# Grouping the tiled matmuls of a four-layer graph kernel: scores, the attends of the pair before, and scores as one block of TensorE

## The chip, the cores and the metric

One NeuronCore of a Trainium2 chip runs the whole program. The metric is device time in microseconds (us) of one execution; medians over several executions are given with their range. The profile is one execution taken with the hardware profiler, whose span is some 2 us shorter than the timed execution.

## The reference

Input `x` is 128 batches of 128 nodes by 512 features in float32, `adj` a 128 x 128 matrix shared by all batches. Four layers follow each other, each with a residual and a layer norm: a graph convolution, a graph attention, a max over differences, and masked multi-head attention. The argument concerns the last one.

```python
# layer 3, per batch: n = 128 nodes, d = 512, H = 8 heads of hd = 64
qkv = (x @ w_qkv).reshape(b, n, 3, H, hd).transpose(2, 0, 3, 1, 4)
q, k, v = qkv[0], qkv[1], qkv[2]
attn = jnp.einsum('bhnd,bhmd->bhnm', q, k) * scale          # "scores"
attn = jnp.where(attn_mask[None, None] == 0, -jnp.inf, attn)
attn = jax.nn.softmax(attn, axis=-1)
o = jnp.einsum('bhnm,bhmd->bhnd', attn, v)                  # "attends"
o = o.transpose(0, 2, 1, 3).reshape(b, n, d) @ w_proj + b_proj
# ... return o + layernorm(o)
```

## The kernel before

The kernel does not write its instructions in the order in which it describes them. Each batch is a generator, a *chain*, that asks for an engine for an estimated time; a planner grants the request that could start first, and the order in which it grants them becomes the fixed order of instructions on each engine. The planner's times decide order alone; on the chip, semaphores decide when each instruction runs.

```python
BUFS = {
    "tr": 3, "mm": 3, "sc": 1,                       # PSUM; sc holds one batch's scores, two banks
    "x": 16, "yT": 3, ..., "v": 8, "qkT": 3, "pr": 2, ...
}

def at(self, r):                                      # earliest start of request r
    engine, _, take, _, _ = r["want"]
    t = max(r["ready"] + (min(MARGIN, r["ready"] / 20) if engine == "PE" else 0.0),
            self.free.get(engine, 0.0))
    ...                                               # and not before its buffers come free
    return t

def run(self):
    while self.requests:
        t, _, _, n = min((self.at(r), r["want"][4], r["rank"], n) for n, r in enumerate(self.requests))
        ...
```

Two batches are a group (`G = 2`). The scores of a batch use 64 rows of the array for each head, the attends 64 columns of it. Everything else (products with the weights, `mixed`, `query_key`) uses the whole 128 x 128 array.

```python
def attend(gr, bs):                                   # both batches of a group together
    for b in bs:
        yield gr.rows[b]                              # transposed probabilities have landed
    slots = yield use("PE", 0.25 + 0.88 * len(bs), lambda: ("tr", "oT") * len(bs), late=0.2, urgent=True)
    for n, b in enumerate(bs):
        valued, prT, bt = gr.heads.pop(b)
        p = bank([P, K, P], "tr")
        for c in range(K):
            for j in range(2):
                nc.tensor.matmul(p[j * HD:(j + 1) * HD, c, :],
                    valued.v[:, (2 * c + j) * HD:(2 * c + j + 1) * HD], prT[:, j * K + c],
                    start=True, stop=True)
    ...

def batch(i):
    ...
    yield gr.qk
    bs = yield use("PE", 1.13, "sc", late=0.2, urgent=True)
    sc = bank([P, 2, K, P], "sc")
    for c in range(K):
        for j in range(2):
            rws = slice(j * HD, (j + 1) * HD)
            nc.tensor.matmul(sc[:, j, c, :], gr.qkT[rws, c, nodes], gr.qkT[rws, K + c, nodes],
                start=True, stop=True)
    bpr = yield use("DVE", 1.22, "pr", urgent=True)
    nc.vector.tensor_tensor(pr, sc..., maskb..., op=ALU.add)     # frees sc
    ...                                               # softmax, 32x32 transposes, two DMAs -> prT
    yield gr.attended[b]
    ...                                               # ACT copy oT, projection, DVE: o, layer norm, out
```

## Time and profile before

| | before |
|---|---|
| time, median of 3 runs | 3310.55 us (3310.03 to 3311.14) |
| span of the profiled execution | 3309.2 us |
| TensorE (PE) busy | 99% |
| VectorE (DVE) busy | 80% |
| waits of TensorE for other engines | 13.4 us in all |

How to read it: TensorE is the path, so busy time of other engines costs nothing as long as TensorE doesn't wait for it. The profile's durations of matmuls overlap (a 512-column instruction is drawn 594 ns long on average, and in a stream the next one starts 429 ns after it), so all readings here subtract **start from start**. A float32 matmul of the source is two instructions in the trace, and in an undisturbed stream one of 512 columns takes 429 ns, one of 256 takes 216 and one of 128 takes 112.

### The profile page before, as it was taken

The page shows a single profiled execution, that of the slowest core. Times are in us where ns is not written, and L with a number is a line of the kernel's source. Part 1 is how long each engine was busy: PE and PEld are TensorE (multiplying, and loading weights), DVE is VectorE, ACT ScalarE, POOL GpSimd, SP SyncE. Part 2 cuts the span into 40 slices and gives each one's busy share as a digit, 9 for nine tenths or more (in the row PEclk, how much of TensorE's full clock was granted, in tenths as well). Part 3 has the DMA queues.
Part 4 walks back from the last instruction along what each step waited for, and adds up shares of the span by engine and source line. Part 5 has one row for each costly group of instructions (what it writes and reads, how often), then busy time and mean ns, then how long its engine had stood idle before and what let it go on. Part 6 is the DMA issues. An engine that isn't in the chain of part 4 may idle for free.

```text
span 3309.2 us, 43603 instructions
## 1 busy us (share of the span) xinstructions
PE 3286.0 (99%) x14613; PEld 2060.0 (62%) x14613; DVE 2640.0 (80%) x5527; ACT 1182.6 (36%) x3457; POOL 935.1 (28%) x1031
## 2 busy tenths in 40 slices
PE   9999999999999999999999999999999999999998
PEld 5666566665656565656666665666565656656655
DVE  7877888768987888787787778886887788778876
ACT  2433244332442333333333333433333334343332
POOL 3222322223222333132233233131331242222322
PEclk9999999999999999999999999999999999999999
DMA  4333223332233232223322332323223332322322
GB/s 163 84 111 100 81 71 101 104 90 91 71 108 96 83 91 88 93 78 101 96 80 91 99 88 88 89 84 113 83 61 116 92 94 72 109 82 71 102 83 80
DMA packets 469760, 304.47 MB, mean 92 GB/s; under 512 B 319264, under 2 KB 401312, under 8 KB 469536
## 3 DMA queue, kind: packets, MB, share of 16 engines
q1 hardware_dynamic: 469536, 301.69, 30.5%
q8 instruction: 116, 1.90, 0.3%
q14 instruction: 108, 0.88, 0.1%
HBM read 158.93 MB, written 142.67 MB: 91 GB/s over the span
## 4 chain that ended last, share of the span: by engine, by line
PE 97%; DVE 2%; DMA 1%; issue 0%; POOL 0%; ACT 0%; SPq 0%; POOLq 0%; ACTq 0%; DVEq 0%
PE mm L199 52%; PE mm L470 27%; PE tr L207 7%; PE sc L625 4%; PE tr L499 4%; PE mm L595 3%; DVE e L442 0%; DMA z<-s_d 0%; DVE st L165 0%; DVE scr L567 0%; DVE x L560 0%; DVE x L186 0%; DMA prT<-p_d 0%; DVE et L445 0%; PE tr L315 0%
## 5 line engine op out<-in xcount | busy, mean ns | idle before, releaser
L199 PE MATMUL mm<-w_sb,yT 128*128 128x512 f32 x2048 | 909.6, 594 | 3.1 <-ACT yT L210 2.0
L470 PE MATMUL mm<-xT,wqkv_sb 128*128 128x256 f32 x4096 | 909.3, 380 | 0.0
L470 PEld LDWEIGHTS mm<-xT,wqkv_sb 128*128 128x128 f32 x4096 | 773.6, 190 | 138.3 <-issue 28.3
L172 POOL TENSOR_TENSOR rstd<-ve,neghalf 128x1 f32<-128x1 f32 x640 | 418.2, 654 | 1528.5 <-DVE ve L169 1241.9
L199 PEld LDWEIGHTS mm<-w_sb,yT 128*128 128x128 f32 x2048 | 381.3, 190 | 451.0 <-issue 434.1
L199 PE MATMUL mm<-wqkv_sb,xT 128*128 128x512 f32 x1024 | 465.9, 598 | 0.0
L199 PE MATMUL mm<-wproj_sb,oT 128*128 128x512 f32 x1024 | 457.4, 596 | 1.5 <-ACT oT L675 1.5
L643 ACT ACTIVATE pr<-pr,nmx 128x128 f32<-128x128 f32 x1024 | 397.7, 391 | 139.9 <-DVE nmx L639 139.2
L165 DVE BATCH_NORM_STATS2 st<-x 128x6 f32<-128x512 f32 x512 | 349.2, 682 | 10.4 <-ACT x L603 7.6
L199 PEld LDWEIGHTS mm<-wproj_sb,oT 128*128 128x128 f32 x1024 | 193.7, 191 | 231.0 <-issue 222.4
L192 POOL TENSOR_TENSOR x<-x,o 128x512 f32<-128x512 f32 x128 | 175.3, 1370 | 533.7 <-DVE o L683 532.6
L199 PEld LDWEIGHTS mm<-wqkv_sb,xT 128*128 128x128 f32 x1024 | 189.1, 190 | 200.3 <-issue 189.8
L181 ACT ACTIVATE x<-x,nmr,rstd 128x512 f32<-128x512 f32 x256 | 205.9, 809 | 279.0 <-DVE nmr L179 270.7
L632 DVE TENSOR_TENSOR pr<-sc,maskb 128x1024 f32<-128x1024 f32 x128 | 156.2, 1220 | 156.1 <-PE sc L625 155.8
L210 ACT COPY yT<-tr 128x512 f32<-128x512 f32 x256 | 148.8, 584 | 262.6 <-PE tr L207 262.2
L192 POOL TENSOR_TENSOR x<-x,beta_sb 128x512 f32<-128x512 f32 x128 | 172.6, 1351 | 201.2 <-DVE xt L609 181.3
L519 ACT COPY v<-mm 128x512 f32<-128x512 f32 x128 | 74.8, 584 | 427.8 <-PE mm L199 427.5
L478 ACT ACTIVATE qkT<-mm 128x512 f32<-128x512 f32 x128 | 76.3, 596 | 371.9 <-PE mm L470 371.8
L192 POOL TENSOR_TENSOR x<-x,bias_sb 128x512 f32<-128x512 f32 x128 | 176.3, 1387 | 106.5 <-PE tr L207 95.8
L567 DVE SCALAR_TENSOR_TENSOR scr<-x,wa_rows 128x512 f32<-128x512 f32 x256 | 195.1, 762 | 13.9 <-ACT x L181 8.8
L643 ACT ACTIVATION_READ_ACCUMULATOR pr<-pr,nmx 128x1 f32 x1024 | 193.4, 189 | 0.0
L625 PEld LDWEIGHTS sc<-qkT 64*128 64x128 f32 x2048 | 124.2, 187 | 81.9 <-issue 65.0
(64 smaller groups left out, 3539.1 us busy)
## 6 DMA issues: line engine op xcount, KB each, us to landing
p_d<-pt SPq DMA_DIRECT2D x128, 512.0 KB
prT<-p_d SPq DMA_DIRECT2D x128, 512.0 KB
x<-in_x SPq DMA_DIRECT2D x128, 256.0 KB
x_d<-xt SPq DMA_DIRECT2D x128, 256.0 KB
xT<-x_d SPq DMA_DIRECT2D x512, 64.0 KB
out<-x SPq DMA_DIRECT2D x128, 256.0 KB
z<-s_d SPq DMA_DIRECT2D x64, 128.0 KB
e_d<-et SPq DMA_DIRECT2D x64, 128.0 KB
```

The costliest lines, as they stand in the source:

```text
L165: nc.vector.bn_stats(st, src)
L172: nc.gpsimd.tensor_tensor(rstd, ve, neghalf, op=ALU.pow)
L181: nc.scalar.activation(xb, xb, AF.Identity, bias=nmr, scale=rstd)
L192: nc.gpsimd.tensor_tensor(dst, dst, other, op=ALU.add)
L199: nc.tensor.matmul(p, lhs(k), rhs(k), start=(k == 0), stop=(k == K - 1))
L207: nc.tensor.matmul(p[:, k, :], xb[:, k * P : (k + 1) * P], nodes, start=True, stop=True)
L210: nc.scalar.copy(yT, p)
L470: nc.tensor.matmul(p[:, j, :], wqkv_sb[:, k, (c + j) * P : (c + j + 1) * P], gr.xT[:, k, :], start=(k == 0), stop=(k == K - 1),)
L567: nc.vector.scalar_tensor_tensor(scr, xb, 1.0, wa_rows[:, j, :], op0=ALU.mult, op1=ALU.mult, accum_out=gr.s[:, b, j : j + 1],)
L625: nc.tensor.matmul(sc[:, j, c, :], gr.qkT[rws, c, nodes], gr.qkT[rws, K + c, nodes], start=True, stop=True,)
L632: nc.vector.tensor_tensor(pr, sc.rearrange("p j c m -> p (j c) m"), maskb[:, None, :].to_broadcast([P, H, P]), op=ALU.add,)
L643: nc.scalar.activation(pr[:, j, :], pr[:, j, :], AF.Exp, bias=nmx[:, j : j + 1], accum_out=sums[:, j : j + 1],)
```

## The change

The intent: the scores of a pair's first batch, the attends of the pair before, and the scores of its second batch follow each other directly, so that the array leaves its whole-array mode once per pair in place of three times. The attends in the middle give VectorE time to empty the only score buffer. A request with `follow=True` goes ahead of others that could start at the same time, and `at()` plans it without its margin (not shown). A block without other work in it is called *undivided* below, and a step from whole-array work into a block an *entry*. Two buffer counts change too. The last eight batches (`TAIL`) keep single scores.

```diff
-    "x": 16, "yT": 3, ..., "v": 8, "qkT": 3,
+    "x": 16, "yT": 4, ..., "v": 6, "qkT": 3,
+TAIL = 8
-        return engine, work, names, late, not urgent
+        return engine, work, names, late, 0 if follow else 1 if urgent else 2
...
+    def tiled(gr, before, bs=range(G)):
+        yield gr.qk
+        if before:
+            for b in range(G):
+                yield before.rows[b]
+        got = yield use("PE", 1.1 if len(bs) == 1 else 1.0,
+            lambda: ("sc",) + ("pr",) * len(bs) + ("tr", "oT") * (G if before else 0),
+            late=0.0, urgent=True)
+        gr.pr.extend(got[1 : 1 + len(bs)])
+        score(gr, bs[0], got[0])
+        if before:
+            yield use("PE", 0.88 * G + 0.15, late=0.0, follow=True)
+            attends(before, range(G), got[1 + len(bs) :])
+        for b in bs[1:]:
+            got = yield use("PE", 1.15, "sc", follow=True)
+            score(gr, b, got)
...
+            if g * G < NB - TAIL:
+                plan.start(tiled(groups[g], groups.get(g - 1)), rank)
+            else:
+                for b in range(G):
+                    plan.start(tiled(groups[g], None, (b,)), rank)
+            if g * G >= NB - TAIL - G:
+                for bs in ((0, 1),) if g * G < NB - G else ((0,), (1,)):
+                    plan.start(attend(groups[g], bs), rank)
... (score() and attends() hold the matmuls of before, unchanged; batch() waits for its scores)
```

More of the change, by code (lines that the diff above doesn't have):

```diff
@@ L30 @@
     "tr": 3, "mm": 3, "sc": 1,
-    "x": 16, "yT": 3, "z": 2, "e": 2, "et": 1, "eT": 2, "ex": 2, "xT": 2, "v": 8, "qkT": 3,
+    "x": 16, "yT": 4, "z": 2, "e": 2, "et": 1, "eT": 2, "ex": 2, "xT": 2, "v": 6, "qkT": 3,
     "pr": 2, "pt": 1, "xt": 2, "prT": 2, "oT": 2, "o": 2,
 }
+TAIL = 8
 MARGIN = 1.0
@@ L56, in __init__, with use @@
         self.now = 0.0
-    def use(self, engine, work, take=None, late=0.05, urgent=False):
+    def use(self, engine, work, take=None, late=0.05, urgent=False, follow=False):
         names = take if callable(take) else lambda: (take,) if take else ()
-        return engine, work, names, late, not urgent
+        return engine, work, names, late, 0 if follow else 1 if urgent else 2
     def start(self, chain, rank):
@@ L90, in at @@
     def at(self, r):
-        engine, _, take, _, _ = r["want"]
-        t = max(r["ready"] + (min(MARGIN, r["ready"] / 20) if engine == "PE" else 0.0), self.free.get(engine, 0.0))
+        engine, _, take, _, order = r["want"]
+        early = min(MARGIN, r["ready"] / 20) if engine == "PE" and order else 0.0
+        t = max(r["ready"] + early, self.free.get(engine, 0.0))
         names = take()
@@ L368, in __init__ @@
             self.rows, self.attended = ([Event() for _ in range(G)] for _ in range(2))
-            self.heads, self.o, self.prT = {}, {}, []
+            self.scored = [Event() for _ in range(G)]
+            self.heads, self.o, self.prT, self.sc, self.pr = {}, {}, [], {}, []
             self.eT, self.xT, self.qkT, self.slot, self.left = {}, None, None, {}, {}
@@ L386, in group @@
                 plan.start(query_key(groups[g], n // 2 * 2 + K * (n % 2)), g * G + n / K - (8 if g * G >= NB - 8 else 0))
-            for bs in ((0, 1),) if g * G < NB - G else ((0,), (1,)):
-                plan.start(attend(groups[g], bs), g * G - (8 if g * G >= NB - 8 else 0))
+            rank = g * G - (8 if g * G >= NB - 8 else 0)
+            if g * G < NB - TAIL:
[6 more added lines that the diff above has]
+                    plan.start(attend(groups[g], bs), rank)
         return groups[g]
@@ L485, in query_key, with score @@
         done(gr.qk)
+    def tiled(gr, before, bs=range(G)):
[3 more added lines that the diff above has]
+                yield before.rows[b]
+        got = yield use(
+            "PE", 1.1 if len(bs) == 1 else 1.0,
+            lambda: ("sc",) + ("pr",) * len(bs) + ("tr", "oT") * (G if before else 0),
+            late=0.0, urgent=True,
+        )
+        gr.pr.extend(got[1 : 1 + len(bs)])
[6 more added lines that the diff above has]
+            score(gr, b, got)
+    def score(gr, b, bs):
+        sc = bank([P, 2, K, P], "sc")
+        nodes = slice(b * P, (b + 1) * P)
+        for c in range(K):
+            for j in range(2):
+                rws = slice(j * HD, (j + 1) * HD)
+                nc.tensor.matmul(
+                    sc[:, j, c, :], gr.qkT[rws, c, nodes], gr.qkT[rws, K + c, nodes],
+                    start=True, stop=True,
+                )
+        gr.read("qkT", G)
+        gr.sc[b] = sc, bs
+        done(gr.scored[b], 0.15)
     def attend(gr, bs):
@@ L490, in attend, with attends @@
         slots = yield use(
-            "PE", 0.25 + 0.88 * len(bs), lambda: ("tr", "oT") * len(bs), late=0.2, urgent=True
+            "PE", 0.25 + 0.88 * len(bs), lambda: ("tr", "oT") * len(bs), late=0.0, urgent=True
         )
+        attends(gr, bs, slots)
+    def attends(gr, bs, slots):
         for n, b in enumerate(bs):
@@ L507, in attend @@
         for b in bs:
-            done(gr.attended[b])
+            done(gr.attended[b], 0.2)
     def values(i, gr, event):
@@ L615, in batch @@
         plan.start(values(i, gr, valued), i + G)
-        yield gr.qk
-        bs = yield use("PE", 1.13, "sc", late=0.2, urgent=True)
-        sc = bank([P, 2, K, P], "sc")
-        nodes = slice(b * P, (b + 1) * P)
-        for c in range(K):
-            for j in range(2):
-                rws = slice(j * HD, (j + 1) * HD)
-                nc.tensor.matmul(
-                    sc[:, j, c, :], gr.qkT[rws, c, nodes], gr.qkT[rws, K + c, nodes],
-                    start=True, stop=True,
-                )
-        gr.read("qkT", G)
-        bpr = yield use("DVE", 1.22, "pr", urgent=True)
-        pr = buf([P, H, P], "pr")
+        yield gr.scored[b]
+        sc, bs = gr.sc.pop(b)
+        yield use("DVE", 1.22, urgent=True)
+        pr, bpr = buf([P, H, P], "pr"), gr.pr.pop()
         nc.vector.tensor_tensor(
```

## The prediction

> **What bounds the kernel now.** I read four views in this order: the page (busy shares and the chain that ended last), the list of waits of TensorE, the instructions in order of time in the middle of the run, and the same at its end. The page first:
>
> ```profile
> PE 3286.0 (99%) x14613; PEld 2060.0 (62%) x14613; DVE 2640.0 (80%) x5527; ACT 1182.6 (36%) x3457; POOL 935.1 (28%) x1031
> ...
> PE 97%; DVE 2%; DMA 1%; issue 0%; POOL 0%; ACT 0%; SPq 0%; POOLq 0%; ACTq 0%; DVEq 0%
> ```
>
> TensorE is busy for 99% of the span and carries 97% of the chain that ended last; VectorE, the next, is busy for 80%. The TensorE waits for other engines add up to 13.4 us in the whole run, 4.6 of them one wait near the end. So time can only go in two places: in what the stream of matmuls itself costs, and in those few waits. A busy share of 99% does not say that the stream is dense, so I read the starts. Middle of the run, TensorE alone; the columns are start, duration, engine, line, operation, tiles, count (each f32 matmul of the source appears as two instructions):
>
> ```profile
> 1507.23 1.97 PE L499 MATMUL tr<-prT,v 128*64 128x128 f32 x32
> 1509.13 3.72 PE L470 MATMUL mm<-xT,wqkv_sb 128*128 128x256 f32 x16
> 1512.68 3.60 PE L199 MATMUL mm<-wproj_sb,oT 128*128 128x512 f32 x8
> 1516.21 1.16 PE L625 MATMUL sc<-qkT 64*128 64x128 f32 x16
> 1517.30 3.70 PE L199 MATMUL mm<-wproj_sb,oT 128*128 128x512 f32 x8
> 1520.93 1.16 PE L625 MATMUL sc<-qkT 64*128 64x128 f32 x16
> ```
>
> Subtract starts, not durations. The scores (sc, 64 rows of the array) and the attends (prT, 64 columns of it) are tiled; all else uses the whole array. In the trace, 512-column instructions that follow each other start 429 ns apart, so eight are 3.43 us. The eight at 1512.68 stand behind whole-array work and in front of a score: 1516.21 - 1512.68 = 3.53, which is 0.10 more. The eight at 1517.30 stand between two scores: 3.63, which is 0.20 more. Going through the starts of the whole trace, these two costs are the same at every place: the last whole-array instruction before a tiled one takes 94 ns more (523 for 429, 309 for 216, 205 for 112), and the first after one takes 104 ns more (533 for 429, 320 for 216). **A visit of whole-array work between two tiled blocks costs 198 ns besides its work.** Within the tiled blocks nothing depends on the neighbour: a score block takes 1092 ns from its first start to the next block's first start in all 128 cases, the 16 behind attends included; an attend block of a pair 1898 ns before a whole-array block and before a score alike.
>
> **The Trainium skill** says in "TensorEngine Tiling (Array Packing)", section Key Properties, that changing the tiling mode drains the TensorE. The trace agrees, and gives a size: 94 + 104 ns around a whole-array visit. By the same sentence score next to attend (row tiles next to column tiles) is a change of mode too; the trace agrees, since the score behind attends still takes 1092 ns, so that boundary is not free, it only lacks the 198. "Perfetto Trace Analysis", section Identifying the Most-Contended Engine, warns that matmul busy share is no measure of headroom; here 198 ns holes are hidden inside a 99%. "TensorE: Matmul & The Clock Gate", Part 1: The HAM clock gate, says that an idle stretch of about 3.4 us halves the clock; the end of the run shows that, below.
>
> **The change, part by part.**
>
> (1) Switches. No matmul is added or removed; the blocks only move. I counted the order of TensorE instructions in both built programs. Entries from whole-array work into tiled work: before 112 into scores and 64 into attends, 176 in all (111 scores and 49 attend blocks stand alone). After: 95 and 6, 101 in all. The intent, scores, attends, scores undivided for each pair, is met in only 33 places; in 26 the block is scores, attends, then other work, then the second scores; 36 scores stand alone, being those second ones and the last groups. So 176 - 101 = 75 visits fewer, each worth 198 ns: **75 x 0.198 = 14.9 us off the path**, all of it on TensorE, which is the path.
>
> (2) The end. The same view there, and the granted clock in windows of it (columns: window, length, busy time and count, clock, DMA share, GB/s):
>
> ```profile
> 3272.60 1.16 PE L625 MATMUL sc<-qkT 64*128 64x128 f32 x16
> 3273.69 7.13 PE L199 MATMUL mm<-wproj_sb,oT 128*128 128x512 f32 x16
> 3285.42 1.44 PE L499 MATMUL tr<-prT,v 128*64 128x128 f32 x16 [4.60 <-DMA prT<-p_d]
> 3287.59 6.30 PE L199 MATMUL mm<-wproj_sb,oT 128*128 128x512 f32 x8 [0.73 <-ACT oT L675]
> 3293.82 1.09 PE L499 MATMUL tr<-prT,v 128*64 128x128 f32 x16
> 3295.66 3.70 PE L199 MATMUL mm<-wproj_sb,oT 128*128 128x512 f32 x8 [0.74 <-ACT oT L675]
> ```
>
> ```profile
> 3280.80:3285.40 4.60, 0.03 (x1) 1.00 0.45 132
> 3285.40:3287.60 2.20, 1.44 (x17) 0.64 0.32 132
> 3287.60:3293.80 6.20, 6.20 (x8) 0.58 0.60 200
> ```
>
> After the last scores only 7.1 us of other work is left, while softmax, transposing and two transfers of the probabilities need 11.7 us (3273.7 to 3285.4): TensorE waits 4.6 us. Then its clock is at 0.58, and eight instructions take 6.2 us in place of 8 x 0.429 = 3.4, so the wait costs 4.6 + 2.7 = 7.3 us. In the changed order, after the last scores stand eight value products, the attends of a pair, four more and eight projection products: 20 source matmuls of 512 columns (two instructions each) at 0.858 us, and 1.9 us, 19.1 us in all. That covers 11.7 us. **I expect the wait and the slow clock behind it to go: 7.3 us.**
>
> (3) A new wait. The scores have one PSUM buffer. In an undivided block the second scores need VectorE to have read the first, while only the attends lie between. From the last start of the first scores: 0.20 to the attends plus 1.90 for them is 2.10 us. VectorE begins the mask addition 0.32 us after that start when it is free (median of 128) and takes 1.22: it ends at 1.54, so 0.56 us is to spare, somewhat less with the signal. In the trace of before, VectorE began over 0.53 us after in a quarter and over 1.02 us in a tenth of the cases; it overruns beyond some 0.8. With 33 such blocks, an estimated 10 to 20% late by some 0.5 us, it costs 2 to 3 us. The 26 divided blocks have no such wait: other work stands there.
>
> (4) Buffers. Six v for eight: at most six products are in v or being made in the changed order, five before, so it fits with nothing over. Attends that wait for the next pair's scores lengthen every batch's life: counted in the order, a median of 11 batches are open, after 9 (most 15, after 14, of 16 x buffers). Adding up matmul durations between the last projection of one batch and the first use of its x buffer by another leaves at least 23 us in the changed order, 74 before. In before, with 74, the earliest use came 64 us after the load's issue; so some 12 us remain in the worst case. Enough, with little over; I put 1 us there. Fourth yT: removes at most the few waits for other work in the middle (1 to 2 us each, three of them); I expect them to come and go, and count 0.
>
> Sum: 3310.6 - 14.9 - 7.3 + 2.5 + 1 = 3291.9; I leave a little for the 2.1 us wait for ScalarE at 3207.7, where more work now stands between, and say **3291 us**.
>
> **The rivals.** (a) The stall in the block takes the gain back. For it: one score buffer, VectorE at 80%, a fixed order that was planned with rounded durations. Were all 33 blocks late by 0.5 us, that is 16 us, and the time is 3305. Against it: the order put other work in the 26 places where the buffer would be late, and the one undivided block of before had no wait. (b) The score-attend boundary costs more than the parts say, since I have 16 cases of attend to score, but only one of score to attend (201 ns, and then the usual attend block). If it hid a drain of 100 ns, 59 such boundaries give 6 us back: 3297. (c) The longer life of a batch starves the first layer of x or the end of work: each stall over 3.4 us also costs clock, as the end of before shows; two would make 3305. (d) The end does not improve, or has another long wait: 3298. None makes VectorE or the DMA queues the bound: their work is unchanged.
>
> **Range and chances.** The 14.9 is counted, and sure within 1 or 2 us unless (b) holds; the 7.3 is likely; the losses are 0 to 10. That gives 3284 to 3301. A change of 2% is 66 us, over four times the switches saved, and a loss of that size would need stalls of 1 us per pair everywhere: 98% for within 2%.
>
> **What will show it.** Fewer entries into tiled work, each still 94 and 104 ns, and attends starting 0.20 us after the last start of scores with no extra; TensorE busy some 15 to 18 us less; no wait of 4.6 us and no clock under 1 at the end; waits of the second scores for the mask addition, a few us in total. Wrong it would be if that wait is frequent, if a wait for the x load or for prT appears in the middle, or if the boundary of scores and attends turns out dear.

## The result

| | before | changed |
|---|---|---|
| time, median of 4 runs | 3310.85 us (3310.03 to 3311.89) | 3292.85 us (3292.42 to 3293.42) |
| span of the profiled execution | 3309.2 us | 3291.2 us |
| ratio | | 0.9946 (0.9928 to 0.9963) |

A ratio here is the mean time of one kernel's fast runs over that of the other's in the same rounds, so it is not quite the ratio of the medians quoted. The time fell by 18.0 us, 0.54%: within 2%, and 1.9 us above the predicted 3291. The output is correct.

The page of the changed kernel, to set against the two lines of before:

```profile
PE 3269.0 (99%) x14613; PEld 2064.7 (63%) x14613; DVE 2663.6 (81%) x5527; ACT 1186.9 (36%) x3457; POOL 965.6 (29%) x1031
...
PE 95%; DVE 3%; DMA 1%; SPq 1%; issue 0%; ACT 0%; POOL 0%; POOLq 0%; DVEq 0%; ACTq 0%
```

The same 14,613 matmuls are busy for 17.0 us less, and the chain that ended last has 3% of VectorE where it had 2%. TensorE in order of time, in the middle of the changed kernel (start, duration, engine, line, operation, tiles, count):

```profile
1464.74 3.62 PE L485 MATMUL mm<-xT,wqkv_sb 128*128 128x256 f32 x16
1468.29 1.16 PE L528 MATMUL sc<-qkT 64*128 64x128 f32 x16
...
1572.45 1.16 PE L528 MATMUL sc<-qkT 64*128 64x128 f32 x16
1573.54 1.97 PE L551 MATMUL tr<-prT,v 128*64 128x128 f32 x32
1575.44 1.16 PE L528 MATMUL sc<-qkT 64*128 64x128 f32 x16
```

An undivided block: 1573.54 - 1572.45 = 1.09 us for the scores and 1575.44 - 1573.54 = 1.90 for the attends. These are the 1092 and 1898 ns that the same blocks took alone. Before a block nothing changed either: 16 instructions at 216 ns are 3.46 us, and 1468.29 - 1464.74 is 3.55, the 94 ns of the entry. The end of the changed kernel, in the same columns:

```profile
3247.20 1.16 PE L528 MATMUL sc<-qkT 64*128 64x128 f32 x16
3248.29 7.13 PE L205 MATMUL mm<-wqkv_sb,xT 128*128 128x512 f32 x16
3255.36 1.97 PE L551 MATMUL tr<-prT,v 128*64 128x128 f32 x32
3257.26 3.70 PE L205 MATMUL mm<-wqkv_sb,xT 128*128 128x512 f32 x8
3260.79 7.03 PE L205 MATMUL mm<-wproj_sb,oT 128*128 128x512 f32 x16
3267.75 1.09 PE L551 MATMUL tr<-prT,v 128*64 128x128 f32 x16
3269.59 3.70 PE L205 MATMUL mm<-wproj_sb,oT 128*128 128x512 f32 x8 [0.74 <-ACT oT L716]
...
3275.05 3.70 PE L205 MATMUL mm<-wproj_sb,oT 128*128 128x512 f32 x8 [0.74 <-ACT oT L716]
```

From 3248.29 to 3267.75 there is 19.5 us of other work behind the last scores, and the attends of the last pair start with no wait. Eight projection instructions take 3.6 us, so the clock is full. The list of TensorE's waits (engine, tile and line, for what, us in total, times, longest) starts with the new one:

```profile
PE sc L528 <- DVE pr L673: 3.0, 3, 1.3
PE mm L205 <- ACT oT L716: 2.1, 3, 0.7
PE tr L213 <- DMA eT<-e_d: 1.5, 1, 1.5
```

Two of the three waits for the mask addition are in undivided blocks (1.36 and 1.35 us by starts, at 1883.3 and 2445.6 us). The third, 0.50 us at 169.4, is in a divided block, where the prediction expected none.

**Where the 18 us went.** I went through all starts of both traces. Each step from start to start was split into its undisturbed length, 94 ns if a tiled block follows, 104 ns if one preceded, and whatever is left (waits and slow clock). All numbers are us of the profiled execution.

| | entries into tiled work | x 0.198 | undisturbed work | waits, slow clock | after the last matmul's start | span |
|---|---|---|---|---|---|---|
| before | 176 | 34.8 | 3243.6 | 18.9 | 10.4 | 3309.2 |
| changed | 101 | 20.0 | 3243.3 | 13.5 | 13.0 | 3291.2 |
| difference | -75 | -14.8 | -0.3 | -5.4 | +2.6 | -18.0 |

(1.4 us before the first matmul is in the span of both.) The undisturbed work is what is left of the time to the last start, so it should agree, as both kernels do the same matmuls. That it does within 0.3 us says that the steps at entries are alike in both traces; it is a check of the bookkeeping and not a test of its own, as a longer step would have been booked as a wait. What tests the 0.198 are the runs below that add and remove entries.

The -5.4 is a net: the wait for the probabilities with its slow clock is gone (-7.6), a wait of 2.2 us for ScalarE shortly before is gone, second scores wait for the mask addition (+3.2 by starts), and some others came (+1.2). The +2.6 was not predicted: from the last matmul's start to the end of the program, the changed kernel takes 13.0 us and the kernel before 10.4.

VectorE at the end of the changed kernel, in order of time:

```profile
3278.71 0.75 DVE L736 SCALAR_TENSOR_TENSOR x<-t,rstd,x 128x512 f32<-128x512 f32 x1
3279.49 0.69 DVE L171 BATCH_NORM_STATS2 st<-x 128x6 f32<-128x512 f32 x1
3280.22 0.18 DVE L173 BATCH_NORM_AGGREGATE mv<-st 128x2 f32<-128x6 f32 x1
3280.44 0.15 DVE L175 TENSOR_SCALAR ve<-mv 128x1 f32<-128x1 f32 x1
3280.51 0.68 DVE L724 TENSOR_TENSOR o<-mm,bproj_sb 128x512 f32<-128x512 f32 x1
3281.32 1.49 DVE L192 TENSOR_SCALAR x<-x,mv,rstd 128x512 f32<-128x512 f32 x1
3282.74 0.68 DVE L171 BATCH_NORM_STATS2 st<-o 128x6 f32<-128x512 f32 x1
```

The last product ends at about 3278.75. Its bias addition (L724) starts at 3280.51, because four VectorE instructions of the batch before stand ahead of it in the fixed order. In the kernel before, the last product ended at 3299.36 and the addition started at 3300.03. From the last matmul's start that is 2.35 us against 1.26, and makes 1.1 of the 2.6 us. The other 1.5 come right after it: the scaling of the batch before (L192) stands between the addition and its statistics, which so begin 2.23 us after the addition's start, and 0.72 us in the kernel before. This scaling took 1.49 us beside an addition to x by GpSimd (3281.27, 1.26 us); in this trace the same operation took 503 to 547 ns in all 211 places where no such addition ran beside it, and up to 1644 ns in the 45 where one did. So part of the gain at the end is lost again in VectorE's order of work.

### The profile page after: what moved, and what is told of

Read it like the earlier page. It is cut to its first block, busy times and chain, and to the rows that moved or that the text cites. A ratio compares the mean times of both kernels' runs of the same rounds, so it can differ in the third digit from the quotient of the medians.

```text
span 3291.2 us, 43479 instructions
## 1 busy us (share of the span) xinstructions
PE 3269.0 (99%) x14613; PEld 2064.7 (63%) x14613; DVE 2663.6 (81%) x5527; ACT 1186.9 (36%) x3457; POOL 965.6 (29%) x1031
## 4 chain that ended last, share of the span: by engine, by line
PE 95%; DVE 3%; DMA 1%; SPq 1%; issue 0%; ACT 0%; POOL 0%; POOLq 0%; DVEq 0%; ACTq 0%
PE mm L205 51%; PE mm L485 27%; PE tr L213 6%; PE sc L528 4%; PE tr L551 3%; PE mm L647 3%; DVE st L171 0%; SPq L589 0%; DMA z<-s_d 0%; DVE x L640 0%; DVE x L192 0%; DVE x L612 0%; DMA s_d<-s 0%; DVE mv L173 0%; DVE pr L691 0%
## 5 line engine op out<-in xcount | busy, mean ns | idle before, releaser
L178 POOL TENSOR_TENSOR rstd<-ve,neghalf 128x1 f32<-128x1 f32 x640 | 444.1, 694 | 1521.8 <-DVE ve L175 1267.0
L205 PE MATMUL mm<-wqkv_sb,xT 128*128 128x512 f32 x1024 | 455.6, 593 | 0.0
L691 DVE TENSOR_TENSOR pr<-pr,rs 128x1024 f32<-128x1024 f32 x128 | 192.0, 1500 | 4.4
```

The costliest lines, as they stand in the source:

```text
L178: nc.gpsimd.tensor_tensor(rstd, ve, neghalf, op=ALU.pow)
L205: nc.tensor.matmul(p, lhs(k), rhs(k), start=(k == 0), stop=(k == K - 1))
L691: nc.vector.tensor_tensor(pr, pr, rs[:, :, None].to_broadcast([P, H, P]), op=ALU.mult)
```

## The experiments

Twelve runs on the chip follow, two of them repeats (r_after is the changed kernel, r_old_buffers is e2_old_buffers). The budget above was drawn up for each, and belongs to all experiments:

| run | entries | x 0.198 | undisturbed | waits, slow clock | after last start | span | time, median |
|---|---|---|---|---|---|---|---|
| e1_buffers | 187 | 37.0 | 3243.4 | 27.8 | 10.1 | 3319.7 | 3321.64 |
| e2_old_buffers | 101 | 20.0 | 3243.6 | 13.4 | 10.1 | 3288.5 | 3288.54 |
| e3_no_follow | 192 | 38.0 | 3243.5 | 24.7 | 10.1 | 3317.7 | 3319.11 |
| e5_split | 223 | 44.2 | 3252.0 | 21.9 | 11.5 | 3330.9 | 3330.63 |
| e6_twice | 178 | 35.2 | 3358.0 | 20.6 | 10.1 | 3425.2 | 3427.0 |
| e7_forced | 76 | 15.1 | 3243.6 | 39.1 | 10.1 | 3309.2 | 3310.00 |
| e8_end | 101 | 20.0 | 3243.5 | 15.7 | 11.4 | 3292.0 | 3291.62 |
| e9_close | 93 | 18.4 | 3243.7 | 14.1 | 11.4 | 3289.0 | 3291.89 |
| r_after | 101 | 20.0 | 3243.4 | 12.5 | 13.0 | 3290.4 | 3292.91 |
| r_old_buffers | 101 | 20.0 | 3243.6 | 10.9 | 10.1 | 3286.0 | 3288.06 |
| e10_end_pair | 100 | 19.8 | 3243.5 | 9.5 | 12.7 | 3286.9 | 3288.63 |
| e11_end_both | 100 | 19.8 | 3243.5 | 9.7 | 12.9 | 3287.3 | 3289.07 |

The theory is that of the prediction: a visit of whole-array work between tiled blocks costs 198 ns, and the gain is the number of visits saved plus the end. The rivals: the buffers do it, the place of the attends does it, or the gaps are no real time.

### The buffers alone, and the order alone

```diff
 # e1_buffers: the kernel before with
-"yT": 3, "v": 8
+"yT": 4, "v": 6
 # e2_old_buffers: the changed kernel with
-"yT": 4, "v": 6
+"yT": 3, "v": 8
```

> The kernel before, with the two buffer counts of the change alone (four yT, six v). Its order has 187 entries from whole-array work into tiled work, against 176 before and 101 after. Theory (the switches and the end make the gain, not the buffers): 11 x 0.198 = 2.2 us slower for the switches, and a longer wait for the probabilities at the end, since only one value product stands after the last scores: some 4 to 8 us more. About 3317 us, 3311 to 3322; each entry still 94 and 104 ns. Rival (the fourth yT takes waits away and makes the gain): 3300 us or less.

> The changed kernel with the old buffer counts (three yT, eight v). Its order again has 101 entries into tiled work, 32 undivided blocks for 33, and the same last steps. Theory: the same time as the changed kernel within 3 us, 3290 to 3296. Rival (the buffers matter): 3300 or more.

The buffers alone made the kernel slower: 3321.64 us (3320.84 to 3321.88), 1.0027 of before (1.0012 to 1.0042). Entries are +2.2 us as counted, and most of the rest is the end, where the wait for the probabilities is 12 us. TensorE there, in order of time:

```profile
3295.93 1.98 PE L499 MATMUL tr<-prT,v 128*64 128x128 f32 x16 [12.00 <-DMA prT<-p_d]
```

The new order with the old buffers took 3288.54 us (3287.65 to 3290.33), ratio 0.9928 (0.9914 to 0.9943), 1.5 us below the expected band. So **the order makes the gain, not the buffer counts**, and with the old counts it is larger. To see whether that difference is real, I ran both on one chip, five rounds each:

> The changed kernel again, on the same chip as the next two, for a fair comparison of the buffer counts. Both theories: 3292.9 us within 2 us.

> The changed kernel with three yT and eight v again. Theory (its 4 us are the 2.9 us of VectorE's order at the end and chance between chips): 2 to 4 us under the changed kernel of this call, in the trace all of it after the last matmul's start, none in entries or waits. Rival (the buffers take waits away): TensorE's last start over 2 us earlier than the changed kernel's.

The changed kernel took 3292.91 us (3291.49 to 3293.12), with the old counts 3288.06 (3287.79 to 3289.56); the ranges do not touch, and the difference is more than the 2 to 4 us expected. In all four traces of the two kernels the part after the last start is 13.0 us with the new counts and 10.1 with the old: 2.9 us. VectorE at the end of e2_old_buffers shows the difference; the last matmul started at 3278.42:

```profile
3279.31 0.68 DVE L724 TENSOR_TENSOR o<-mm,bproj_sb 128x512 f32<-128x512 f32 x1
3280.03 0.69 DVE L171 BATCH_NORM_STATS2 st<-o 128x6 f32<-128x512 f32 x1
```

The addition starts 0.89 us after it (2.35 in the changed kernel), and its statistics follow directly. **TensorE has no long wait at the end here either, so the changed kernel's longer end is not the price of the removed wait.** It comes with the order that the plan gave VectorE under the new counts.

The last start itself came 0.3 us later with the old counts in the first pair of traces and 1.5 us earlier in the second. Two differences repeat in both pairs and nearly cancel: by starts, scores wait 0.1 us for the mask addition with the old counts and 3.2 and 2.4 us with the new; in the list of waits, products wait 3.8 and 3.7 us for yT with the old counts and 0.7 with the new. One does not repeat: in e2_old_buffers the clock record reaches full rate at 10.5 us and not at 5.0 as in r_old_buffers, which cost it 1.5 us (e3_no_follow and e8_end have the same). The remainder is in waits that differ from run to run, and is not settled.

### Dividing the blocks again

```diff
-        return engine, work, names, late, 0 if follow else 1 if urgent else 2
+        return engine, work, names, late, 1 if follow or urgent else 2
```

> The changed kernel where the attends and the second scores are asked for as ordinary urgent work, so that whole-array work comes between them: 192 entries into tiled work for 101, one block for 33. Theory: 91 x 0.198 = 18.0 us slower, less the 3.2 us that second scores waited for the mask addition; and its end has one value product after the last scores, so the wait for probabilities comes back there, with the slow clock, some 5 to 10 us: about 3317 us, 3308 to 3322; in the trace 18.0 us of it in starts around entries. Rival (what gained was the place of the attends in the order and the end, not the missing entries): the TensorE stream up to 3200 us into the run is no longer than in the changed kernel by more than 4 us, and the total is under 3303.

Measured: 3319.11 us (3317.33 to 3319.51), inside the expected band. Everything else of the change is kept (the margin of `at()` comes back with the edit), and 18.0 us come back in entries; the "undisturbed" column stays at 3243.5. Another 11 us come back in waits, nearly all of it one: the last scores of this order have one value product behind them, and TensorE waits 12.0 us for the probabilities, followed by slow-clock instructions:

```profile
PE tr L551 <- DMA prT<-p_d: 12.0, 1, 12.0
```

The total alone does not rule out the rival that only the place of the attends mattered, as this wait is part of it. The trace does: what the changed kernel's TensorE has done by 3200.0 us, this one, measured by undisturbed lengths, has done by 3215.1, where the rival allowed 4 us.

### More entries on purpose

```diff
 # the kernel before, with the attends of each batch asked for apart
-for bs in ((0, 1),) if g * G < NB - G else ((0,), (1,)):
+for bs in ((0,), (1,)):
```

> The kernel before with the attends of the two batches of each pair asked for apart: 223 entries into tiled work for 176, 124 attend blocks for 65. Theory: 47 x 0.198 = 9.3 us for entries, and each further attend block has its own first gap (50 ns more) and last gap (99 ns more), 59 x 0.149 = 8.8 us; with a longer wait at the end of some 4 to 8 us about 3335 us, 3328 to 3340. Rival (these starts are how the profiler draws matmuls, and no time lies in them): 3311 to 3319.

Measured: 3330.63 us (3329.15 to 3332.71), inside the expected band. The 47 further entries cost 9.3 us, and the 59 further attend blocks raised the undisturbed column by 8.4 us, where 8.8 was expected. Sixteen-instruction attend blocks take 1024 ns from start to the next block's start, in front of whole-array work and of scores alike. If the gaps were only drawn by the profiler, the time would have stayed near 3311 to 3319. They are time.

### Twice the same mode

```diff
 # the kernel before: each batch's eight score matmuls issued twice, over the same buffer (still correct)
-        for c in range(K):
+        for c in list(range(K)) * 2:
```

> The kernel before with each block of scores computed twice in a row (the same eight matmuls again, over the same buffer; the result stays right), to see whether tiled work behind tiled work of the same mode pays anything. Theory (the extra gaps belong to a change of mode, not to a new group of matmuls): the second eight take 8 x 112 = 896 ns, blocks of 1988 ns for 1092, the stream 128 x 0.896 = 114.7 us longer. Rival (each group of eight pays its own first and last gap): blocks of 2184 ns, 139.8 us. In both cases the end of this order has one value product after the last scores, and so some 8 us more of wait: about 3434 us in the first, 3459 us in the second.

One look: 3427.0 us, state unknown. TensorE in the middle, in order of time:

```profile
1521.40 2.06 PE L625 MATMUL sc<-qkT 64*128 64x128 f32 x32
1523.38 3.70 PE L199 MATMUL mm<-wqkv_sb,xT 128*128 128x512 f32 x8
1527.01 2.06 PE L625 MATMUL sc<-qkT 64*128 64x128 f32 x32
1529.00 1.27 PE L207 MATMUL tr<-eT,x 128*128 128x128 f32 x9
```

A doubled block takes 1.98 us (1985 ns in all 128 cases): 893 more, not 1092. So tiled work behind tiled work of the *same* mode pays nothing, and a block's own extra (1092 - 8 x 112 = 196 ns) belongs to the change of mode. That the second eight use the same operands and buffer is not the reason: the attends of a pair are two batches with two buffers, and their block of 1898 ns is also shorter than two of 1024 (e5_split). Scores next to attends keep that part and lose only the 198 ns.

### Forcing the blocks together

Only 33 of 59 blocks with attends are undivided, because the planner puts other work in where it sees the score buffer come free late. This run lets the second scores follow anyway.

```diff
+    def key(self, r):
+        t, free = self.at(r), self.free.get(r["want"][0], 0.0)
+        return free if r["want"][4] == 0 and t - free < 1.0 else t
...
-                (self.at(r), r["want"][4], ...
+                (self.key(r), r["want"][4], ...
+            t = self.at(r)
```

> The changed kernel, where the second scores of a block may be placed directly after the attends even if the plan sees the score buffer come free up to 1 us late: 76 entries into tiled work for 101, 57 undivided blocks for 33. Theory (a late buffer costs more than the entry that it saves): 25 x 0.198 = 5.0 us saved, but the second scores then wait for the mask addition, 10 to 18 us in total for 3.2; and its end has 8.8 us of work after the last scores for 19.1, so the wait for the probabilities is there again with the slow clock, some 8 us. About 3308 us, 3299 to 3315. Rival (the plan divided too often, the real buffer is in time): waits of second scores under 5 us in total, and without the end's wait a stream shorter than that of the changed kernel by 3 us or more.

Measured: 3310.00 us (3308.31 to 3311.87). Its two largest waits of TensorE:

```profile
PE tr L556 <- DMA prT<-p_d: 12.8, 1, 12.8
PE sc L533 <- DVE pr L678: 8.4, 10, 2.2
```

Entries fell by 5.0 us. Second scores waited 8.4 us in this list, for 3.0 in the changed kernel; by starts it is 10.0 in 17 places, the lower edge of the 10 to 18 expected. By the starts, without the end's 17.7 us (12.9 of wait, a slow clock and two copies by ScalarE), 21.4 us of waits are left; the changed kernel has 11.9 without its two copies. So the forced blocks save 5.0 and the waits rise by 9.5, part of them waits for other things that moved. Dividing a block where the buffer is late was right in this order.

### The end

```diff
 # e8_end: the changed kernel; plans the last bias addition earlier in VectorE's order
-        bp = yield use("PE", 3.46, "mm", late=0.2)        # projection
+        bp = yield use("PE", 3.46, "mm", late=0.2 if i < NB - 1 else -1.8)
 # e9_close: old buffer counts, the line above, and key() as above with 0.15 us, in the first 2000 us
```

> The changed kernel with one thing moved: VectorE's bias addition to the last projection product is placed in VectorE's order ahead of the last statistics of the batch before it. Theory (the 2.6 us more that the changed kernel needs after its last matmul come from VectorE's order there, as the last product now ends while VectorE is busy with the batch before): 1.0 to 1.8 us less after the last matmul's start than the 13.0 of the changed kernel, so about 3291.4 us. Rival (the chain of the last batch itself is what takes that time): 13.0 us as before, 3292.9.

> A try for a better version: the changed kernel with the old buffer counts, a plan that places the second scores directly after the attends when their buffer is at most 0.15 us late (in the first 2000 us only), and the last bias addition moved up as in the run on the end. 93 entries into tiled work for 101. Theory: 8 x 0.198 = 1.6 us less for entries, under 1 us of new waits, and an end like that of the kernel with the old buffers (10.1 us after the last start) or better: 3286 to 3289. Rival (buffer waits eat it, or other waits come): 3290 or more.

e8_end took 11.4 us after the last start in place of 13.0: the expected 1.0 to 1.8 us. Its time, 3291.62 us (3288.82 to 3293.75), agrees with the expected 3291.4, but the runs scatter over more than the effect; the profiled execution had 2.2 us more waits elsewhere (a stretch of 3.4 us at half the clock, behind a wait of 1.9 us at 1885, cost it 1.7 us, and a late full clock at the start 1.6; other waits were shorter). What is shown is the trace's 1.6 us. e9_close saved its 1.6 us of entries, but had an end of 11.4 us where the kernel with the old counts has 10.1 without it, and other waits: 3291.89 us (3289.28 to 3295.55), no better, as its rival said.

```diff
 # e10_end_pair: old buffer counts, and the last pair's attends as one block
-for bs in ((0, 1),) if g * G < NB - G else ((0,), (1,)):
+for bs in ((0, 1),):
 # e11_end_both: e10_end_pair, with late=-1.0 for the last projection
```

> The kernel with the old buffer counts, where the attends of the very last pair are one block too, in place of two with a projection between: 100 entries into tiled work for 101, 64 attend blocks for 65, one wait for ScalarE's copy of 0.81 us for two. Theory: 0.81 + 0.20 + 0.15 = 1.2 us less than the kernel with the old buffer counts in this call. Rival (VectorE's work on the last two batches is the end's bound): no less.

> The kernel with the last pair's attends as one block and the old buffer counts, and with VectorE's bias addition to the last product placed ahead of the scaling of the batch before it. TensorE's order is unchanged by it. Theory (VectorE's order at the end takes back what TensorE saved): after TensorE's last start 10.5 to 11.5 us for 12.7, and so 1 to 2 us less, 3286.5 to 3287.6 where the kernel without it had 3288.6; the best of all. Rival (two batches' work on VectorE does not fit in less): 12.7 us and 3288.6 again.

Both failed as tries for a faster kernel, and the rivals held. In e10_end_pair the TensorE stream is 1.7 us shorter (last start at 3274.2 for 3275.9, on the same chip), with no wait for ScalarE's copy between the last products, and the time is 3288.63 us (3288.33 to 3289.00) for 3288.06. VectorE shows why:

```profile
3274.88 0.84 DVE L733 SCALAR_TENSOR_TENSOR t<-o,mv,gamma_sb 128x512 f32<-128x512 f32 x1
3276.16 0.75 DVE L736 SCALAR_TENSOR_TENSOR x<-t,rstd,x 128x512 f32<-128x512 f32 x1 [0.44 <-POOL rstd L178]
3276.83 0.68 DVE L724 TENSOR_TENSOR o<-mm,bproj_sb 128x512 f32<-128x512 f32 x1
```

The last product is there by some 3274.9, and its addition starts at 3276.83, behind the scaling of the batch before. In e11_end_both that addition was moved up and starts at 3275.01, but the end is no shorter: 12.9 us, 3289.07 us (3288.10 to 3290.58, another chip). VectorE now works from there on at two batches at once, and one instruction of it takes twice its time, beside an addition by GpSimd (3275.78, 1.70 us). In the changed kernel's trace this operation took 750 to 754 ns in all 96 places without such an addition beside it, and 1564 ns in the median of the 32 with one:

```profile
3275.01 0.68 DVE L724 TENSOR_TENSOR o<-mm,bproj_sb 128x512 f32<-128x512 f32 x1
3275.61 0.74 DVE L733 SCALAR_TENSOR_TENSOR t<-o,mv,gamma_sb 128x512 f32<-128x512 f32 x1
3276.46 1.56 DVE L736 SCALAR_TENSOR_TENSOR x<-t,rstd,x 128x512 f32<-128x512 f32 x1
```

So with the last pair as one block TensorE no longer bounds the end: its 1.7 us are worth nothing, and the work that VectorE and GpSimd still have, with the output's transfer behind it, fills the last 13 us. Of all kernels run, the changed order with the old buffer counts has the lowest median, 3288.06 us, 0.9932 of before (0.9918 to 0.9945); the two tries lie within 1.0 us of it, too near to be told apart.

## Why the prediction was right or wrong

It was right: 3292.85 us for 3291, within the range, and the change is within 2%. The main mechanism is shown; that the total is within 1.9 us is partly luck, since losses that the sum lacked (2.6 us after the last matmul, 1.2 of other waits, 0.7 more for scores) were in part made up by 1.0 us for buffers that was not needed, 1.3 more from the wait for ScalarE and some 0.6 of smaller terms.

- **The switches, -14.9 us: right, and shown.** The changed trace has exactly 101 entries, each still 94 + 104 ns. Twelve traces with 76 to 192 entries leave the same undisturbed work within 0.4 us; the other two are the kernels with more tiled blocks or more tiled work on purpose. In device time, e3_no_follow and e5_split give the cost back.
- **Scores next to attends, rival (b): wrong rival, the theory held.** There was one case in the trace before; now 59 steps from scores to attends take 202 ns and the attends their usual 1898.
- **The end, -7.3 us: right.** The wait and the slow clock are gone (-7.6 by starts). That it takes enough work behind the last scores is shown from the other side too: e1_buffers and e3_no_follow have 3.6 us there and e7_forced 8.8, and they wait 12.0 to 12.8. But the 11.7 us that the probabilities need was one sample: from the end of the last scores to the attends it is 15.7 us in e1_buffers (3280.24 to 3295.93), 15.7 in e3_no_follow and 21.8 in e7_forced. The 19 us would not have covered the last; what makes that length differ is not settled.
- **The stall of the second scores, +2 to 3 us: right as a sum, and by luck.** The list of waits has 3.0 us in 3 places. The prediction had 10 to 20% of the 33 blocks late by some 0.5 us; 2 of 33 were, by 1.35 us, and a divided block added 0.5. All 33 blocks late, rival (a), did not happen.
- **Buffers, +1 us, and the fourth yT, 0:** no wait for a load of x is in TensorE's list of the changed kernel, so that 1 us was not needed. What the buffer counts did was not foreseen: with the old counts the same order is faster by 4.8 us, 2.9 of it at the end, though it waits 3 us more for yT.
- **What failed: the sum has no term for what follows the last matmul.** I took the end's 7.3 us as whole gain, and the step from the last matmul to the end of the program as unchanged. It took 13.0 us for 10.4, so 2.6 us came back: VectorE's order puts work of the batch before ahead of the last addition and between it and its statistics. e8_end, which changes this order alone, takes 1.6 us of it back; the kernel with the old counts, which has no wait at the end either, needs 10.1 us. The 2.2 us wait for ScalarE that I left "a little" for did go, and hid that miss in the total.

## What to carry to other kernels

Count how often a busy TensorE changes its tiling mode: here each visit of whole-array work between tiled blocks costs 0.2 us that no wait shows and that only start-to-start differences reveal; placing blocks of small matmuls next to each other saves it, as long as the buffer between them is free in time. Where it is not, other work in the gap is cheaper than a wait. At the end of a program read what the next engine does: here time saved on TensorE was worth only what VectorE's fixed order let through.

## What the Trainium skill lacked or had wrong

- "TensorEngine Tiling (Array Packing)", Key Properties, says that a mode change drains the TensorE, but gives no size. Here, for float32: 94 ns before a tiled block and 104 ns after it, and inside the block 101 ns (row tiles) or some 50 ns (column tiles) on one of its first steps and 97 to 100 ns on its last. Row tiles next to column tiles pay the inner part (202 ns in the step, 1092 and 1898 ns blocks unchanged) and not the 198; the same mode twice pays nothing (1985 ns for two blocks of scores).
- "TensorE: Matmul & The Clock Gate", Part 2, Step-by-step, says that weight loads are pulled ahead of running matmuls. It names conditions for it, but not that it stops at a mode change or a wait. In the trace before, in a stream the load of the next weights starts with the matmul in front; at the change to scores both start together at 1516.21, and back at 1517.30, and behind the wait at 841.98. The 104 ns on the first step also follow waits with no mode change (533 ns for 429 after the waits at 842.0 and 2418.6 us).
- The same page, Back-to-back issue gap, gives no float32 times. Here a float32 matmul is two instructions of 429 ns each for 512 columns, 216 for 256 and 112 for 128.
- The same page, Part 1: The HAM clock gate, gives an idle stretch of about 3.4 us for the fall to half the clock. The trace before agrees: 853 ns for 429 after a wait of 4.6 us. But shorter stretches did it too: in e1_buffers (3079 us), e7_forced (800), e8_end (1885) and e9_close (3085) TensorE was idle for 1.9 to 2.2 us, and the clock record then has half the rate for 3.4 us. Idle stretches of 2.1 us (before, 3205) and 3.0 us (e5_split, 3292) did not, nor any of 1.3 to 1.8 us; so the length alone does not decide here.
- On return to full clock the same section says about 3.4 us of work; the four stretches above agree. At the end of the trace before, the half rate lasted from 3286.0 to 3292.9 us, with a second gap of 0.7 us in between, so longer than that.
